# Layer 0 of a four-layer convolution network: x in pairs of patch rows, and one load for both the first block and the first image's statistics

## The chip, the cores and the metric

The kernel runs on one core of a Trainium2 chip. The metric is the device time of one execution in microseconds (us), as the median of several executions. All times before the change are of the same kernel file, and "the profile" is one execution of it that was recorded by the hardware profiler.

## The reference

Four residual layers follow each other on a tensor x of shape (4, 64, 256, 256), float32. Only layer 0 is touched:

```python
x = x + _L0_conv_ref(_gn(x), w_in, w_dw, fft_filter, w_out)   # layer 0
x = x + _L1_conv_ref(_gn(x), kernel)                          # layer 1
x = x + _L2_conv_ref(_gn(x), core, periphery, threshold, scale, 1, 1)
x = x + _L3_conv_ref(_gn(x), weights1, weights2)

def _L0_conv_ref(x, w_in, w_dw, fft_filter, w_out):           # p = 8
    x = jnp.einsum('bchw,oc->bohw', x, w_in)                  # 64 -> 384 channels
    xp = x.reshape(B, C, H // p, p, W // p, p).transpose(0, 1, 2, 4, 3, 5)
    xf = jnp.fft.rfft2(xp) * fft_filter                       # per 8x8 patch
    xp = jnp.fft.irfft2(xf, s=(p, p))
    x = xp.transpose(0, 1, 2, 4, 3, 5).reshape(B, C, H, W)
    x = lax.conv_general_dilated(x, w_dw, (1, 1), [(1, 1), (1, 1)], feature_group_count=C)
    x1, x2 = jnp.split(x, 2, axis=1)
    return jnp.einsum('bchw,oc->bohw', jax.nn.gelu(x1, approximate=False) * x2, w_out)
```

`_gn` subtracts the mean of a group of two channels over a whole image and divides by the root of its variance, so nothing of an image can be normalized before the whole image has been read once.

## The kernel before, in words

**Start.** The 256 image rows are 32 patch rows of 8 rows each. The statistics of image 0 are read in 32 parts of 512 KB (`first_stats`, L663). Tensor `flat` lays each part over all 128 partitions: partition 2c+s holds half s of channel c, 4096 bytes in a run, one DMA for a part. Seven buffers (`p_s`) rotate, so part k+7 is asked for when part k has been read. VectorE reads each part with two `bn_stats` (`input_stats`, L320). Between them stands, at k = 0, 10 and 20, the building of the depthwise-and-FFT weights: `tables` on VectorE (L339 to L352), copies into the tiles `T` on ScalarE and GpSimd (L391) and twelve writes of `T` to HBM from GpSimd's queue (L395). Then `group_norm` gives scale and shift; as `flat` mixes channels differently from the working layout it uses two averaging matrices (`c_avgp`, `c_avgx`). Tile `u` takes the memory of the weight tiles when these are done.

**Blocks.** An image is three blocks of 11 output patch rows; twelve blocks in all. A block needs patch rows i0 to i0+11, of which one is shared with the block before it. i0 is -1, 10 or 21, so the first block of an image has no row t = 0 and the last one has no row t = 11. `load_x` reads one patch row as two DMAs (L418): partitions 0 to 63 get the left half of the image's width, 64 to 127 the right half, in runs of 512 bytes. `normalize_x` scales it into a tile `xn` (L256 on ScalarE; in block 0 every other row on GpSimd, L425).

**The four passes of a block.** For each of four groups kb of 96 hidden channels the kernel first expands (`expand`) every patch row t into `u`, then runs the patch convolution on `u` (`own` L498, `beside` L514) for twelve pairs of channel groups g, with GELU on ScalarE (L521), the product on VectorE (L522) and the result to HBM (L525, tile `g`). An expand step has two forms: for t < 6 ("pairs") 16 matmuls of 128 weights columns (L446) and four copies on each of ScalarE and VectorE (L461); for t of 6 and more 32 matmuls of 64 columns (L452) and three copies on each (L463 to L465). The profile counts each matmul twice[...].

**Units.** While block p convolves, the projection of block p-1 is done in 16 units (`project`, L602, L609), four in each pass, at g = 0, 4, 6, 8 in the pass kb = 0 and g = 0, 2, 6, 8 in the others. A unit adds into a residual tile `r` (loaded by `load_r`, L570) and asks for the next row's `r` and `g` (`load_half`, L557, L561).

**Order.** TensorE, VectorE, ScalarE and SyncE run in the order in which the program is written (`manual_schedule`); GpSimd's order follows from it. All loads of layer 0 stand on SyncE's queue (SP), which waits in order for the buffers it loads into. `load_w` (L473, four buffers) waits for TensorE and so keeps SP in step with the convolution. The statistics of the next image (L638) and the x of the next block share the four buffers `p_x`; in passes kb 0 to 2 up to four statistics parts a pass are loaded, at the end of kb = 2 four rows of x (g = 8 and g = 10), and in pass kb = 3 the next block's rows are normalized, three ahead of g = 0 and two after each pair of groups.

Of the kernel before, what the change touches and what calls it, by code (L numbers as in the profile page):

```python
# [17 lines left out]
C = 64  # L18
# [3 lines left out]
GROUPS = 32  # L22
# [47 lines left out]
def _constants(H, W):  # L70
# [4 lines left out]
    grpp = np.arange(128) // 2 // (C // GROUPS)  # L75
    avgp = (grpp[:, None] == grpp[None, :]) / np.sum(grp == 0)
    avgx = (grpp[:, None] == grp[None, :]) / np.sum(grp == 0)
# [10 lines left out]
        "c_ident": np.eye(128), "c_avg32": avg32, "c_sel32": sel32, "c_kext": _patch_kernel(), "c_avg": avg, "c_avgp": avgp, "c_avgx": avgx,  # L88
# [33 lines left out]
class _Net:  # L122
# [152 lines left out]
    def _layer0(self, ctx, dst):  # L275
# [32 lines left out]
        p_xn, p_x = pool("l0xn", NR + 1), pool("l0x", 4)  # L308
# [20 lines left out]
        p_s = ctx_a.enter_context(tc.tile_pool(name="l0as", bufs=7))  # L329
# [46 lines left out]
        def weights(t, copies):  # L376
# [33 lines left out]
        rows_of = lambda p: [  # L410
            (blocks[p][0], blocks[p][1] + t) for t in range(NR + 1) if 0 <= blocks[p][1] + t < NP
        ]

        def load_x(row, p_x=p_x):
            b, i = row
            x0[row] = p_x.tile([128, P, HW2], F32, tag="x", name=f"x0_{b}_{i}")
            for s in range(2):
                nc.sync.dma_start(x0[row][halves[s]], a["x"][b, :, P * i : P * i + P, s * HW2 : (s + 1) * HW2])  # L418

        def normalize_x(row, pool=False):  # L420
            b, i = row
            xn = xns[row] = p_xn.tile([128, HW2 // P, P, P], F32, tag="xn", name=f"xn_{b}_{i}")
            to, x = xn.rearrange("p m r w -> p r m w"), x0.pop(row).rearrange("p r (m w) -> p r m w", w=P)
            if pool:
                nc.gpsimd.tensor_scalar(to, x, self.r[0][:, b : b + 1], self.nb[0][:, b : b + 1], ALU.mult, ALU.add)  # L425
            else:
                self.normalize(to, x, 0, b)
# [6 lines left out]
        def expand(p, kb, t):  # L434

            b, i0 = blocks[p]
            ps = [banks(f"psu_{p}_{kb}_{t}_{s}") for s in range(2)]
            xn = xns[b, i0 + t]
            lo, hi = halves
            pairs = t < (NR + 1) // 2  # L440
# [15 lines left out]
            at = lambda h, o: u[h, :, t * CW + o : t * CW + o + 8].rearrange("p c (s m) -> p c s m", s=2)  # L456
            for s, copy in enumerate((nc.scalar.copy, nc.vector.tensor_copy)):
                v = ps[s][:, :, 0 : 8 * PB].rearrange("p s (m c) -> p c s m", m=4)
                if pairs:
                    for h, o, k, c in ((lo, O1, lo, 0), (hi, O2, lo, PB), (lo, E1 + 1, hi, 0), (hi, E2 + 1, hi, PB)):  # L460
                        copy(at(h, 8 * s + o), v[k, c : c + PB])  # L461
                    continue
                copy(at(slice(0, 128), 8 * s + 1), v[:, 0:PB])  # L463
                copy(at(hi, 8 * s + E2 + 1), v[lo, PB:])
                copy(at(lo, 8 * s + O1), v[hi, PB:])  # L465
# [186 lines left out]
        with ordered:  # L652

            bst0 = new_bst0(0)
            flat = a["x"][0].rearrange("c (s h) w -> (c s) (h w)", s=2)
            avgs = [self.load(name, p_a) for name in ("c_avgp", "c_avgx")]
            parts = {}

            def first_stats(k):
                if k >= NJ:  # L660
                    return
                t = parts[k] = p_s.tile([128, 4, W], F32, tag="x", name=f"st_{k}")
                nc.sync.dma_start(t.rearrange("p r w -> p (r w)"), flat[:, 4 * W * k : 4 * W * (k + 1)])  # L663
# [5 lines left out]
            for k in range(7):  # L669
                first_stats(k)  # L670
            copies = [nc.scalar.copy, nc.gpsimd.tensor_copy, nc.scalar.copy]
            for k in range(NJ):
# [4 lines left out]
                first_stats(k + 7)  # L677
            rows = rows_of(0)
            for row in rows[:4]:
                load_x(row)  # L680
            for j in range(3):
                load_w(j)
            self.group_norm(0, 0, bst0, avgs)
            ctx_a.close()

            p_1, p_6 = (pool(n, 2, side="right") for n in ("l0g1", "l0g6"))
            p_r = pool("l0r", 2, side="right")
# [3 lines left out]
            sources = [[p_1, p_6, p_r]]  # L691
# [831 lines left out]
```

## Time and profile before

| what | value |
|---|---|
| median of three runs (lowest, highest) | 6424.22 us (6414.56, 6427.8) |
| the profiled execution: its own time / its span | 6435.86 us / 6434.0 us |
| TensorE matmul busy | 5962.3 us, 93% of the span |
| VectorE / ScalarE / GpSimd busy | 4271.5 / 3239.1 / 1058.2 us |
| moved by DMA | 1448.20 MB, mean 225 GB/s, 879566 packets |
| statistics of image 0 end on VectorE (start of L200) | 90.42 us |
| first normalized row starts on ScalarE (L256) | 99.54 us |
| first expand matmul of block 0 (L446) | 100.83 us |
| convolution of block 0 runs without gaps from (L498) | 149.72 us |

Times in the views are counted from the start of the span. A timeline line gives start, duration, engine, source line, operation, output and inputs, how many instructions were merged, and in brackets how long the engine had been idle before it and what ended that. In a table of stretches the columns are start:end, length, busy time of each engine with its instructions, the TensorE clock that was granted, the share of the 16 DMA engines' time that was busy, and GB/s. A line of waits gives the total in us, how often, and the longest. "issue" is a wait for nothing that the profile shows.

### The profile page before, as it was taken

The numbers are of one execution on the slowest core, as the hardware profiler recorded it, in microseconds if no ns is written. First come the engines' busy times: TensorE is split into PE (matmuls) and PEld (weight loads), VectorE is DVE, ScalarE is ACT, GpSimd is POOL, SyncE is SP. The second block draws the span as 40 slices with busy tenths as digits, with TensorE's granted clock in tenths as the row PEclk, the third lists the DMA queues.
The fourth block names the chain that finished last, engine by engine and source line by source line (L and its number), as shares of the span: only waits on it lengthen the run. The fifth ranks groups of instructions, "written<-read, shape, count | busy, mean of one in ns | idle before, by whom it ended". The sixth has DMA issues, their size and how long they took to land.

```text
span 6434.0 us, 238132 instructions
## 1 busy us (share of the span) xinstructions
PE 5962.3 (93%) x106712; PEld 3313.0 (51%) x106712; DVE 4271.5 (66%) x5924; ACT 3239.1 (50%) x4560; POOL 1058.2 (16%) x1651
## 2 busy tenths in 40 slices
PE   3999999999999999999999969999899999999997
PEld 2565555555555555555565533333344444443566
DVE  5566565565666565655565538999788988885264
ACT  3454444444344444343444406777777877773211
POOL 4111111111111111111111111111122222221011
PEclk9999999999999999999999979999999999999855
DMA  8587888888888878887877699999566666678899
GB/s 237 161 216 217 225 234 240 240 230 227 243 225 236 228 210 236 239 233 219 227 207 211 196 233 240 229 228 229 139 174 176 177 169 172 169 187 286 302 365 393
DMA packets 879566, 1448.20 MB, mean 225 GB/s; under 512 B 77284, under 2 KB 587508, under 8 KB 876500
## 3 DMA queue, kind: packets, MB, share of 16 engines
q1 hardware_dynamic: 726340, 923.62, 55.7%
q0 software_dynamic: 148672, 500.14, 23.0%
q8 instruction: 843, 13.81, 0.9%
q10 hardware_dynamic: 3536, 9.20, 0.6%
q14 instruction: 175, 1.43, 0.1%
HBM read 932.61 MB, written 500.04 MB: 223 GB/s over the span
## 4 chain that ended last, share of the span: by engine, by line
PE 76%; DMA 9%; DVE 8%; ACT 3%; issue 3%; SPq 0%; POOL 0%; DVEq 0%; ACTq 0%; POOLq 0%
PE pc L514 16%; PE pc L498 11%; PE m L906 10%; PE one L1147 9%; PE div L1106 7%; DVE u L461 5%; PE psu L446 5%; PE psu L452 5%; PE po L602 4%; DMA g<-g 2%; PE psz L1136 2%; DMA x<-in_x_dram 2%; PE po L609 2%; DMA x<-x 2%; PE psa L1334 2%
## 5 line engine op out<-in xcount | busy, mean ns | idle before, releaser
L522 DVE TENSOR_TENSOR h<-h,pc 128x374 f32<-128x374 f32 x1152 | 575.7, 541 | 1171.1 <-ACT h L521 1171.0
L521 ACT ACTIVATE h<-pc 128x374 f32<-128x374 f32 x1152 | 494.0, 480 | 1649.4 <-PE pc L514 1649.0
L514 PE MATMUL pc<-u,w 64*16 64x374 f32 (+2 forms) x27648 | 1179.3, 479 | 1.9 <-issue 1.9
L525 POOL DMA_DIRECT2D g<-h x576 | 418.4, 726 | 2874.5 <-DVE h L522 2784.7
L498 PE MATMUL pc<-u,w 64*64 64x374 f32 x9216 | 828.8, 483 | 14.0 <-DVE r L623 5.1
L514 PEld LDWEIGHTS pc<-u,w 64*16 64x16 f32 (+2 forms) x27648 | 466.8, 92 | 678.8 <-issue 638.0
L461 DVE COPY u<-psu 64x384 f32<-64x384 f32 x1088 | 605.0, 556 | 60.6 <-PE psu L446 42.5
L1092 DVE TENSOR_TENSOR q<-xn 128x2313 f32<-128x2313 f32 (+2 forms) x256 | 627.6, 2493 | 1.7 <-ACT xn L256 1.7
L446 PE MATMUL psu<-win,xn 64*128 64x96 f32 x8704 | 588.7, 279 | 42.0 <-ACT u L461 21.6
L461 ACT COPY u<-psu 64x384 f32<-64x384 f32 x1088 | 559.3, 514 | 115.5 <-PE psu L446 90.8
L1147 PE MATMUL one<-z,wp 32*32 32x512 f32 x16384 | 595.7, 597 | 21.7 <-issue 17.5
L452 PE MATMUL psu<-win,xn 64*64 64x96 f32 x17408 | 502.0, 256 | 118.2 <-issue 75.2
L446 PEld LDWEIGHTS psu<-win,xn 64*128 64x128 f32 x8704 | 553.7, 190 | 97.8 <-DVE h L522 30.7
L256 ACT ACTIVATE xn<-x,nb,r 128x1024 f32<-128x1024 f32 (+3 forms) x268 | 478.4, 1799 | 246.0 <-DMA x<-x 140.4
L498 PEld LDWEIGHTS pc<-u,w 64*64 64x64 f32 x9216 | 360.4, 132 | 389.0 <-issue 165.7
L1093 ACT ACTIVATE q<-q 128x2313 f32<-128x2313 f32 (+2 forms) x256 | 528.9, 2086 | 31.9 <-DVE q L1092 31.0
L452 PEld LDWEIGHTS psu<-win,xn 64*64 64x64 f32 x17408 | 438.6, 140 | 176.7 <-issue 101.3
L1147 PEld LDWEIGHTS one<-z,wp 32*32 32x32 f32 x16384 | 368.2, 103 | 229.9 <-issue 88.2
L1106 PE MATMUL div<-q,ones 64*32 64x512 f32 x8192 | 471.0, 601 | 10.1 <-ACT q L1093 9.3
L1180 POOL DMA_DIRECT2D x<-r x512 | 274.3, 544 | 980.0 <-DVE r L1177 946.8
L602 PE MATMUL po<-g,wo 128*64 128x176 f32 (+1 forms) x3072 | 320.1, 351 | 75.6 <-DMA g<-g 51.3
L906 PE MATMUL m<-t,wk 64*64 64x512 f32 x3072 | 341.2, 588 | 0.0
(163 smaller groups left out, 6703.2 us busy)
## 6 DMA issues: line engine op xcount, KB each, us to landing
g<-h POOLq DMA_DIRECT2D x576, 374.0 KB, 6.9
x<-x SPq DMA_DIRECT2D x240, 640.0 KB, 6.5
w<-wt SPq DMA_DIRECT2D x288, 448.0 KB, 6.7
x<-x SPq DMA_DIRECT2D x100, 1024.0 KB, 14.3
g<-g SPq DMA_DIRECT2D x414, 187.0 KB, 6.5
g<-g SPq DMA_DIRECT2D x736, 93.5 KB, 6.0
x<-in_x_dram SPq DMA_DIRECT2D x258, 256.0 KB, 8.6
x<-o POOLq DMA_DIRECT2D x128, 512.0 KB, 8.3
```

What stands on the lines that cost most here:

```text
L446: nc.tensor.matmul(ps[s][:, k, at], xn[halves[s], n : n + 2].rearrange("p n r w -> p (n r w)"), win[halves[s], kb, 0 : 2 * PB], start=True ...
L452: nc.tensor.matmul(ps[s][halves[1 - odd], k, at], xn[halves[s], n + odd].rearrange("p r w -> p (r w)"), win[halves[s], kb, PB * (1 - odd) ...
L461: copy(at(h, 8 * s + o), v[k, c : c + PB])
L498: nc.tensor.matmul(out(C * c, C, k, h), w[halves[h], k, 2 * (G % 2) + c, 0:C], cells(h, 4 * g + 2 * k + c, 0, 0), start=True, stop=False, ...
L514: nc.tensor.matmul(out(q, m, k, h), w[halves[h], k, 2 * (G % 2) + c, c0 : c0 + m], cells(h, 4 * g + 2 * k + c, down, right), start=False, ...
L522: nc.vector.tensor_mul(h[:, k], h[:, k], ps[k][:, 1, 0:L])
L602: nc.tensor.matmul(out(k, s, x), wo1, moving(g1[:, 2 * k], 2 * half + k, s, x), start=(x == 0), stop=False, skip_group_check=True,)
L906: nc.tensor.matmul(rows2(m)[halves[j], s], w[dx][halves[s]], ts[n][halves[s], i, 2 * j : 2 * j + 2, dx : dx + W], start=(dx == 0), stop=(d ...
L1092: nc.vector.tensor_sub(d, p0, p1)
L1093: nc.scalar.activation(d, d, AF.Square)
L1106: ins = nc.tensor.matmul(ps[quarters[j], h], ones[halves[h]], q[n, g, k][halves[h], r + 2 * j : r + 2 * j + 2, o : o + W], start=(m == 0), ...
L1147: ins = nc.tensor.matmul(rows2(ps[g])[quarters[j], k], w[quarters[i]], z[quarters[i], h, 2 * j + dy : 2 * j + dy + 2, dx : dx + W], tile_p ...
```

## The change

**Layout of x.** A part of x is now four image rows of two neighbouring patch rows: partitions 0 to 63 hold rows of patch row i, partitions 64 to 127 the same rows of patch row i+1, each over the whole width, 4096 bytes in a run. Two parts (k = 0, 1) make a pair of patch rows. The last patch row of a block (k = 2, the one shared with the next block) keeps the old layout, in a pool `p_x1` of its own. A part is 512 KB as before, in two DMAs of 64 partitions.

**Expand.** A step of a block is now the left or right half of a pair of patch rows, so a step fills half of two rows of `u` rather than one whole row. `pairs` goes by the number of the step in the block (under 6), not by t: a block with i0 = -1 now has six steps with pairs and five without, where it had five and six. The other two kinds of block keep their numbers (six and six, six and five).

**Start.** The first ten statistics parts of image 0 are the ten parts of block 0 (`kept`), and stay in SBUF (four in `p_x`, six in a temporary pool `p_f`) until they are normalized. The other 22 parts rotate in three buffers, not seven, and are laid out like the later images' statistics: two DMAs of 64 partitions a part. All 32 parts have the working layout, so `group_norm` uses one matrix. The reload of block 0's rows is gone, but for the shared row (k = 2). Two parts on ScalarE and two on GpSimd are normalized before the first step, and one more at each later step.

**Loads.** The first unit in pass kb = 0 moves from g = 0 to g = 4 (now g = 4, 6, 8, 10). The first two `load_half` move from t = 0 and t = 11 to t = 11 and g = 0, and the `load_r` of the first row from the end of the block before to step t = 0. Two of the four x loads at the end of pass kb = 2 move into pass kb = 3, behind its expand steps.

```diff
-        p_xn, p_x = pool("l0xn", NR + 1), pool("l0x", 4)
+        p_xn, p_x1, p_x = pool("l0xn", NR // 2), pool("l0x1", 2), pool("l0x", 4)
...
-        p_s = ctx_a.enter_context(tc.tile_pool(name="l0as", bufs=7))
+        p_s = ctx_a.enter_context(tc.tile_pool(name="l0as", bufs=3))
+        ctx_f = ExitStack()
+        p_f = ctx_f.enter_context(tc.tile_pool(name="l0f", bufs=6, side="right"))
...
+        def parts_of(p):
+            b, i0 = blocks[p]
+            out = [(b, i0 + 1 + 2 * m, k) for m in range(NR // 2) for k in range(2)]
+            return out + ([(b, i0 + NR, 2)] if i0 + NR < NP else [])
+        def load_x(part, p_x=p_x):
+            b, i, k = part
+            x0[part] = t = p_x.tile([128, 4, W], F32, tag="x", name=f"x0_{b}_{i}_{k}")
             for s in range(2):
-                nc.sync.dma_start(x0[row][halves[s]], a["x"][b, :, P * i : P * i + P, s * HW2 : (s + 1) * HW2])
+                if k < 2:
+                    nc.sync.dma_start(t[halves[s]], a["x"][b, :, P * (i + s) + 4 * k : P * (i + s) + 4 * k + 4, :])
...
+        def steps_of(p):
+            b, i0 = blocks[p]
+            one = lambda t: [(b, i0 + t, 0, [(t, 0), (t, 1)])] if 0 <= i0 + t < NP else []
+            out = one(0)
+            for t in range(1, NR, 2):
+                out += [(b, i0 + t, q, [(t, q), (t + 1, q)]) for q in range(2)]
+            return out + one(NR)
-        def expand(p, kb, t):
-            pairs = t < (NR + 1) // 2
+        def expand(p, kb, step, pairs):
+            b, i, q, to = step
+            xn = xns[b, i][:, 16 * q : 16 * q + 16]
...
             for s, copy in enumerate((nc.scalar.copy, nc.vector.tensor_copy)):
+                o0 = to[s][0] * CW + 8 * to[s][1]
...
-            flat = a["x"][0].rearrange("c (s h) w -> (c s) (h w)", s=2)
-            avgs = [self.load(name, p_a) for name in ("c_avgp", "c_avgx")]
+            first_parts = parts_of(0)
+            kept, parts = first_parts[: 2 * (NR // 2)], {}
             def first_stats(k):
+                if k < len(kept):
+                    load_x(kept[k], p_x if k < 4 else p_f)
+                    parts[k] = x0[kept[k]]
+                    return
                 t = parts[k] = p_s.tile([128, 4, W], F32, tag="x", name=f"st_{k}")
-                nc.sync.dma_start(t.rearrange("p r w -> p (r w)"), flat[:, 4 * W * k : 4 * W * (k + 1)])
+                for s in range(2):
+                    nc.sync.dma_start(t[halves[s]], src_t[0, :, k, s])
...
-            for k in range(7):
+            for k in range(len(kept) + 3):
                 first_stats(k)
...
-                first_stats(k + 7)
-            rows = rows_of(0)
-            for row in rows[:4]:
-                load_x(row)
+                if k >= len(kept):
+                    first_stats(k + 3)
...
-            self.group_norm(0, 0, bst0, avgs)
+            self.group_norm(0, 0, bst0)
...
                 def load_next(kb):
-                    if kb < 3 and nk:
+                    if kb == 3:
+                        load_rows(2)
+                    elif nk:
...
                     for t in range(NR + 1):
+                        if p == 0 and kb == 0:
+                            if t == 1:
+                                for part in first_parts[len(kept) :]:
+                                    load_x(part)
+                            for n in range(4) if t == 0 else range(t + 3, t + 4):
+                                if n < len(first_parts):
+                                    normalize_x(first_parts[n], pool=n % 2 == 1)
+                        if t < len(steps):
+                            expand(p, kb, steps[t], t < (NR + 1) // 2)
+                        if t == 0 and kb == 0 and 0 < p:
+                            load_r(p - 1, 0)
-                        if t in (0, NR) and first:
-                            load_half(*first.pop(0))
                         if t == NR:
+                            if first:
+                                load_half(*first.pop(0))
                             load_w(p * (HID // 8) + NG * kb // 2 + 3)
                             load_next(kb)
...
-                        if g in (0, 2 if kb else 4, 6, 8):
+                        if g in ((0, 2, 6, 8) if kb else (4, 6, 8, 10)):
                             unit()
-                        if g < 6:
+                        if g == 0 and first:
+                            load_half(*first.pop(0))
+                        if g < 6 and kb < 3:
                             load_next(kb)
...
-                            if g == NG - 2 and p < NB - 1:
-                                load_r(p, 0)
...
-                        if kb == 2 and g >= NG - 4:
+                        if kb == 2 and g == NG - 2:
                             load_rows(2)
```

## The prediction

> **What bounds the kernel now.** I read the page first, then the timeline of the first 155 us, then TensorE's waits and its timeline inside layer 0, then tables of short stretches for the DMA rates.
>
> ```profile
> PE 5962.3 (93%) x106712; PEld 3313.0 (51%) x106712; DVE 4271.5 (66%) x5924; ACT 3239.1 (50%) x4560; POOL 1058.2 (16%) x1651
> ...
> PE 76%; DMA 9%; DVE 8%; ACT 3%; issue 3%; SPq 0%; POOL 0%; DVEq 0%; ACTq 0%; POOLq 0%
> ```
>
> TensorE is the bound nearly everywhere. So a change of loads can gain only where TensorE stands still: at the start, and in short gaps inside the blocks.
>
> ```profile
> 6.47 64.82 SPq L663 DMA_DIRECT2D st<-in_x_dram  x32
> ...
> 47.94 1.29 DVE L320 BATCH_NORM_STATS2 bst<-st 128x6 f32<-128x512 f32 x2 [3.54 <-DMA st<-in_x_dram]
> ...
> 71.35 29.18 SPq L418 DMA_DIRECT2D x<-in_x_dram  x8
> ...
> 90.42 1.89 DVE L200 BATCH_NORM_AGGREGATE mv<-bst 128x2 f32<-128x384 f32 x1
> ...
> 99.54 1.24 ACT L256 ACTIVATE xn<-x,nb,r 128x1024 f32<-128x1024 f32 x1 [19.29 <-DMA x<-in_x_dram]
> ...
> 149.72 2.81 PE L498 MATMUL pc<-u,w 64*64 64x374 f32 x28 [1.22 <-DVE u L465]
> ```
>
> The statistics wait for their DMAs and end at 90.4 us; ScalarE then waits for x that is read a second time, and block 0's first expand pass (100.83 to 149.72, 49 us) goes row by row with these loads. The same pass in kb = 1 takes 25 us.
>
> ```profile
> PE psu L452 <- issue: 66.3, 49, 5.7
> ```
>
> ```profile
> 722.75 2.95 PE L452 MATMUL psu<-win,xn 64*64 64x96 f32 x64 [4.93 <-issue]
> ```
>
> ```profile
> q1 hardware_dynamic: 2162, 2.32, 87.4%
> q8 instruction: 3, 0.05, 1.7%
> ```
>
> Inside the blocks the largest gap of TensorE is no data wait: 66.3 us of "issue" in the expand steps with 64-column matmuls. The last two lines are the DMA view of 711 to 724 us, around the gap that the timeline line shows: loads fill the engines while instruction packets of 16 KB come on queue 8. I read it as late instructions; it is an inference. From the timeline, gaps over 0.9 us add up to 3.9 us a block in pass kb = 0, 1.9 in kb = 3, and almost nothing in the two others.
>
> [...]in 110 to 120 us the granted clock is 0.66 and 64 matmuls take 6.73 us, against 3.81 later.
>
> ```profile
> 9.00:20.00 11.00, 0.00 (x0) 0.00 (x0) 11.00 (x19) 5.42 (x27) 7.75 (x20) 1.00 1.00 390
> 121.00:129.00 8.00, 6.42 (x96) 6.06 (x96) 3.55 (x7) 3.50 (x8) 1.20 (x1) 0.61 0.88 180
> 131.00:138.00 7.00, 4.31 (x123) 4.12 (x119) 3.34 (x6) 4.19 (x7) 0.00 (x0) 0.74 0.61 152
> ```
>
> The last two columns are the busy share of the DMA engines and GB/s. Statistics parts over 128 partitions: 390 GB/s with all engines busy. Rows of x in two halves, 512-byte runs: 180 / 0.88 = 205. Statistics parts of image 1 in two halves, 4096-byte runs: 152 / 0.61 = 249. So the longer run is worth a fifth, and the half-wide tile costs a third or more. The new layout is the third row, and it also replaces the first.
>
> **The change part by part.**
>
> *Statistics stage, slower.* A part took 0.524 MB / 390 = 1.34 us alone and, from the stats starting at 47.94, 50.63 and 53.19, 2.6 us beside the writes of T. In halves it takes 0.524 / 249 = 2.1 us alone. Beside the writes it lies between 2.6 (the writes are the limit) and 2.6 x 390 / 249 = 4.1 (all of it is the halves); I take 3.0. Parts 0 to 5 land by 20 us, part 9 at 20 + 4.5 x 3.0 = 33.5, so the second `tables` (9.7 us long, from 26.34 before) runs 34.7 to 44.4. With three buffers only parts 10 to 12 are loaded meanwhile. Part 13 is asked for when part 10 is read (45.6), lands 3.5 + 1 us later (3.47 is the shortest landing of a half), then one per 3.0 us: part 19 is read at 69.7, `tables` ends at 79.4, part 23 lands at 85, part 31 at 109. Statistics end at 110 instead of 90.4. With 2.6 us a part the same walk gives 102, with 3.6 it gives 121; above that the writes run out and the reads speed up.
>
> *Start of block 0, faster.* From the end of the statistics to scale and shift took 5.3 us (90.4 to 95.7); two matmuls and a copy less, 5.0. GpSimd's queue then holds the memset of u (1.47) ahead of its first normalization (1.20), and the first step needs both parts: TensorE starts 7.7 us after the statistics. The pass has six steps with pairs and five without: ScalarE does 6 x 2.13 + 5 x 1.54 of copies and four normalizations of 1.24 between them, 25.4 us, after a cold first step of 3.3: 29 us, where x loads made it 49. The convolution starts at 110 + 7.7 + 29 = 146.7, 3.0 us earlier than 149.72 (bounds: 11 earlier, 8 later). The reload of 5.2 MB that is saved pays for the slower reads and little more.
>
> *Expand form, slower.* In four blocks one step of eleven changes from three copies and 64-column matmuls to four copies and 128-column ones. The timeline prices them:
>
> ```profile
> 1160.47 6.81 PE L446 MATMUL psu<-win,xn 64*128 64x96 f32 x96 [0.48 <-ACT u L461]
> ...
> 1171.61 6.73 PE L452 MATMUL psu<-win,xn 64*64 64x96 f32 x252 [0.17 <-DVE u L465]
> ```
>
> Three pair steps take 6.81 + 0.08 of overlap, 2.28 a step (VectorE's four copies of 0.556 are 2.22); four of the other kind take 6.73, 1.7 to 1.85 with their waits. So 0.45 us x 15 passes (block 0's first is in the sum above) = 7 us more; from 4 to 13, since whole passes with six pairs end 23.2 to 23.4 us after their start and those with five 22.1 to 22.7.
>
> *Unit moved from g = 0 to g = 4, faster.* Gaps of the convolution in pass kb = 0 of blocks 1 to 10 add up to 6.7 us; with g loaded half a pass earlier most of them go: 4 us less (0 to 6). VectorE's adds (1.46 + 0.80 + 0.80) move beside matmuls either way.
>
> *Loads inside blocks.* 110 of the 117 later rows of x change from 512 to 4096 bytes, about a fifth less engine time on 58 MB of the 668 MB that the DMA view counts from 100 to 3100 us. SP issues as many DMAs. Moved on SP: `load_r` of the first row passes only g loads that wait for the block's last `g` write, so it starts when it did; the `r` of the second row leaves the crowded expand of kb = 0, while a statistics part enters it; two x parts in kb = 3 now stand behind a `load_w` that waits for TensorE to end the pass before, so they land within the expand rather than ahead of it. Who waits behind them: the normalization at g = 0, some 20 us later, which a landing of 8 to 13 us leaves room for. For the late instructions I take 5 us less, between 33 less (half of 66) and 22 more (kb = 3 gets gaps like kb = 0's, 2.0 more in 11 blocks).
>
> *Costed at nothing:* the normalization's new write order (runs of 8 floats as before, 1.24 us); `p_f` and the later pools over it (first used in block 1). Layers 1 to 3 only start earlier or later.
>
> **Sum.** -3 + 7 - 4 - 5 = -5 us on the profiled 6435.86 us (span 6434.0). That execution lies 11.6 us above the median of the runs; I carry the difference to the median: 6424.2 - 5 = 6419 us. About 0.2% (13 us) is what a measurement here can tell from no change.
>
> **Rivals.**
> - *Instruction gaps shrink by half* (faster): x in 4096-byte runs and the second `r` out of the way. -3 + 7 - 4 - 33 = -33: 6391 us. For it: nearly every long gap of kb = 0 follows `r` and statistics loads. Against: as many bytes are moved in the same passes.
> - *The x parts moved into kb = 3 collide with its 64-column steps* (slower). Place: the second half of that expand, where instructions are used up fastest. Price: 2.0 us x 11 = 22, without the 5 saved: -3 + 7 - 4 + 22 = +22, 6446 us. It decides from (13 + 0) / 11 = 1.2 us a block on. For it: the gaps of kb = 3 already follow x loads. Against: half of these loads stood close by before.
> - *The halves cost little at the start or a lot:* at 3.6 us a part, 121 instead of 110: +11 on the sum, 6430 us. This is also the case in which the change does not do what it says, since the longer runs then buy nothing.
>
> **Chances.** Likeliest case 0.45 (own range 6404 to 6434), gaps halve 0.25, collision 0.20, slow statistics 0.10. Faster: 0.25 and an eighth of the likeliest case, 0.30. Slower: 0.20 and some of the two middle cases, 0.26. Range 6386 to 6448, which leaves out the far ends of both outer rivals.
>
> **What would show it.** Right: L200 starts near 110 us (102 to 121), `st` and first x DMAs at about 250 GB/s when alone, the first pass of block 0 some 29 us long without x waits on ScalarE, its convolution at about 147; L446 rises from 8704 to 9216 matmuls; "issue" at the 64-column line near 60 us. Wrong: L200 before 98[...], or "issue" under 35 or over 80.

## The result and the profile after

The kernel after takes 6440.15 us (median of 20 runs, 6424.17 to 6447.08), the kernel before on the same chip 6421.69 us (20 runs, 6407.66 to 6440.3). The ratio is 1.0026, 95% interval 1.0019 to 1.0034: slower by 0.26%, some 17 us. The profiled execution has a span of 6445.2 us against 6434.0.

The page of after, engines and chain:

```profile
PE 5961.0 (92%) x106198; PEld 3303.0 (51%) x106198; DVE 4282.4 (66%) x5939; ACT 3245.7 (50%) x4575; POOL 1059.0 (16%) x1651
...
PE 76%; issue 7%; DVE 7%; DMA 6%; ACT 3%; POOL 1%; SPq 0%; POOLq 0%; DVEq 0%; ACTq 0%
```

TensorE does the same work in the same busy time. So the loss is again in its waits, and in the chain the share of DMA has even fallen (9% to 6%) while that of issue rose (3% to 7%).

The timeline of the start of after (L317 reads the parts, L692 loads the 22 that are not kept, L197 ends the statistics):

```profile
5.54 15.85 SPq L422 DMA_DIRECT2D x<-in_x_dram  x20
22.02 90.15 SPq L692 DMA_DIRECT2D st<-in_x_dram  x44
...
41.20 3.65 DVE L317 BATCH_NORM_STATS2 bst<-st 128x6 f32<-128x512 f32 x6
49.68 1.29 DVE L317 BATCH_NORM_STATS2 bst<-st 128x6 f32<-128x512 f32 x2 [4.82 <-DMA st<-in_x_dram]
...
62.02 1.29 DVE L317 BATCH_NORM_STATS2 bst<-st 128x6 f32<-128x512 f32 x2 [5.64 <-DMA st<-in_x_dram]
...
73.34 1.29 DVE L317 BATCH_NORM_STATS2 bst<-st 128x6 f32<-128x512 f32 x2 [3.42 <-DMA st<-in_x_dram]
...
90.02 1.28 DVE L317 BATCH_NORM_STATS2 bst<-st 128x6 f32<-128x512 f32 x2 [2.15 <-DMA st<-in_x_dram]
...
118.68 1.29 DVE L317 BATCH_NORM_STATS2 bst<-st 128x6 f32<-128x512 f32 x2 [1.27 <-DMA st<-in_x_dram]
120.00 1.89 DVE L197 BATCH_NORM_AGGREGATE mv<-bst 128x2 f32<-128x384 f32 x1
...
157.65 2.81 PE L523 MATMUL pc<-u,w 64*64 64x374 f32 x28 [0.81 <-DVE u L490]
```

The statistics end at 120.0 us (before 90.4). Block 0's first expand pass then takes 30 us where it took 49, and its convolution runs without gaps from 157.65, 7.9 us later than before. Alone, the parts in two halves came about as fast as forecast, 241 GB/s against 249 (last two columns: busy share of the DMA engines, GB/s):

```profile
9.00:20.00 11.00, 0.00 (x0) 0.00 (x0) 11.00 (x18) 5.21 (x27) 7.66 (x20) 1.00 1.03 241
```

For the blocks I took from TensorE's timeline, for each pass, the time from its first expand matmul to its first convolution or projection matmul, and from there to the next pass. The table has the means of blocks 1 to 9 in us:

| kernel | kb = 0 | kb = 1 | kb = 2 | kb = 3 | block |
|---|---|---|---|---|---|
| before | 28.3 + 51.0 | 24.0 + 50.4 | 23.8 + 50.5 | 26.8 + 50.9 | 305.7 |
| after | 28.4 + 54.3 | 25.4 + 50.3 | 23.8 + 50.3 | 24.4 + 49.4 | 306.1 |

So two things of about equal size cancel in each block: kb = 0 and 1 lose 4.7 us, kb = 3 gains 4.0. TensorE's waits between 100 and 3100 us in after name the loss (in the columns: total, times, longest):

```profile
PE psu L476 <- issue: 47.4, 45, 3.1
PE psu L470 <- ACT u L486: 21.0, 42, 1.3
PE pc L523 <- DVE u L490: 18.1, 18, 2.0
PE pc L539 <- issue: 11.1, 9, 2.2
```

"Issue" at the 64-column matmuls fell from 66.3 to 47.4. The third line is new in this size (3.9 before): the convolution's first matmuls wait for VectorE's last copy into `u`. So is the fourth (1.9 before), a wait inside the convolution for nothing that the profile shows.

### The profile page after: what moved, and what is told of

Same layout as the page of the kernel before. It is cut to its first block, busy times and chain, and to the rows that moved or that the text cites. A ratio compares the mean times of both kernels' runs of the same rounds, so it can differ in the third digit from the quotient of the medians.

```text
span 6445.2 us, 237146 instructions
## 1 busy us (share of the span) xinstructions
PE 5961.0 (92%) x106198; PEld 3303.0 (51%) x106198; DVE 4282.4 (66%) x5939; ACT 3245.7 (50%) x4575; POOL 1059.0 (16%) x1651
## 4 chain that ended last, share of the span: by engine, by line
PE 76%; issue 7%; DVE 7%; DMA 6%; ACT 3%; POOL 1%; SPq 0%; POOLq 0%; DVEq 0%; ACTq 0%
PE pc L539 17%; PE pc L523 11%; PE m L940 10%; PE one L1181 9%; PE div L1140 7%; PE psu L470 4%; DVE u L486 4%; PE psu L476 4%; PE po L627 4%; PE psz L1170 2%; PE po L634 2%; DMA x<-x 2%; PE psa L1368 2%; ACT u L486 1%; DMA g<-g 1%
## 5 line engine op out<-in xcount | busy, mean ns | idle before, releaser
L539 PE MATMUL pc<-u,w 64*16 64x374 f32 (+2 forms) x27648 | 1186.2, 479 | 12.5 <-issue 12.5
L523 PE MATMUL pc<-u,w 64*64 64x374 f32 x9216 | 835.8, 485 | 28.3 <-DVE u L490 21.1
L539 PEld LDWEIGHTS pc<-u,w 64*16 64x16 f32 (+2 forms) x27648 | 465.7, 92 | 698.5 <-issue 664.1
L486 DVE COPY u<-psu 64x384 f32<-64x384 f32 x1152 | 640.1, 556 | 50.6 <-PE psu L470 31.3
L470 PE MATMUL psu<-win,xn 64*128 64x96 f32 x9216 | 618.3, 277 | 36.1 <-ACT u L486 24.9
L486 ACT COPY u<-psu 64x384 f32<-64x384 f32 x1152 | 592.3, 514 | 109.8 <-PE psu L470 78.7
L470 PEld LDWEIGHTS psu<-win,xn 64*128 64x128 f32 x9216 | 582.0, 188 | 93.3 <-ACT u L486 33.6
L476 PE MATMUL psu<-win,xn 64*64 64x96 f32 x16384 | 468.5, 253 | 89.0 <-issue 55.3
L476 PEld LDWEIGHTS psu<-win,xn 64*64 64x64 f32 x16384 | 407.3, 138 | 145.7 <-issue 83.2
L627 PE MATMUL po<-g,wo 128*64 128x176 f32 (+1 forms) x3072 | 316.3, 348 | 64.8 <-DMA g<-g 37.9
```

Of the source, the lines that this page charges most:

```text
L470: nc.tensor.matmul(ps[s][:, k, at], xn[halves[s], n : n + 2].rearrange("p n r w -> p (n r w)"), win[halves[s], kb, 0 : 2 * PB], start=True ...
L476: nc.tensor.matmul(ps[s][halves[1 - odd], k, at], xn[halves[s], n + odd].rearrange("p r w -> p (r w)"), win[halves[s], kb, PB * (1 - odd) ...
L486: copy(at(h, o0 + o), v[k, c : c + PB])
L523: nc.tensor.matmul(out(C * c, C, k, h), w[halves[h], k, 2 * (G % 2) + c, 0:C], cells(h, 4 * g + 2 * k + c, 0, 0), start=True, stop=False, ...
L539: nc.tensor.matmul(out(q, m, k, h), w[halves[h], k, 2 * (G % 2) + c, c0 : c0 + m], cells(h, 4 * g + 2 * k + c, down, right), start=False, ...
L627: nc.tensor.matmul(out(k, s, x), wo1, moving(g1[:, 2 * k], 2 * half + k, s, x), start=(x == 0), stop=False, skip_group_check=True,)
```

## The experiments

Each kernel was timed beside the kernel before on its own chip, in five rounds. The chips differ by 0.4% (before took 6421 to 6445 us), so kernels are compared with after by the quotient of their ratios; its uncertainty is some 0.15%, or 10 us. My theory: the start is slower because the half-wide loads are slow, and moving the unit uncovers the copies into `u`. Rivals: the loss is in the blocks alone (pairs form, instruction gaps); only the number of buffers counts at the start.

| kernel | ratio to before (95%) | against after, us |
|---|---|---|
| one DMA a part (`e_one_start`) | 1.0388 (1.037 to 1.0407) | +232 |
| eight parts ahead (`e_deep`) | 0.9986 (0.9976 to 0.9996) | -26 |
| unit back at g = 0 (`e_unit0`) | 0.9959 (0.9946 to 0.9973) | -43 |
| five pairs where it had five (`e_pairs`) | 1.0027 (1.0015 to 1.0039) | +1 |
| before, unit moved (`b_unit_only`) | 1.0069 (1.0054 to 1.0084) | |
| before, halves (`b_halves`) | 1.0026 (1.0014 to 1.0037) | |
| both repairs (`e_best`) | 0.9921 (0.9907 to 0.9936) | -67 |
| fill in one quarter (`e_fill`) | 1.0074 (1.006 to 1.0088) | +31 |
| fill in four quarters (`e_fill2`) | 1.0005 (0.9995 to 1.0014) | -13 |
| x loads early (`e_xearly`) | 1.0031 (1.0021 to 1.004) | +3 |
| three pairs (`e_pairs3`) | 1.0074 (1.006 to 1.0087) | +31 |
| all pairs (`e_allpairs`) | 1.0094 (1.0081 to 1.0108) | +44 |
| after, short runs (`e_short`) | 1.0059 (1.0046 to 1.0072) | +21 |
| before, long runs (`b_long`) | 0.9956 (0.9942 to 0.9969) | |

### The start: halves or buffers

`e_one_start`:

```diff
+        def load_both(t, b, row, apart):
+            v = a["x"][b, :, row : row + 4, :]
+            src = bass.AP(tensor=v.tensor, offset=v.offset, ap=[[apart * W, 2], [H * W, C], [1, 4 * W]])
+            nc.sync.dma_start(t.rearrange("p r w -> p (r w)"), src)
...
-                for s in range(2):
-                    nc.sync.dma_start(t[halves[s]], src_t[0, :, k, s])
+                load_both(t, 0, 8 * k, 4)
```

> The kernel after, with one edit: each of the 32 statistics parts of image 0, the ten kept ones included, is read by one DMA over all 128 partitions and not by two of 64; places, buffers (three) and everything else stay. My theory (halves are what makes the statistics stage slow): the statistics end at 94 to 100 us, not at 120.0, block 0's convolution runs from about 135, not 157.65, and the time falls by about 20 us (15 to 25) below the kernel after, to about its 6420. Rival (only the small number of buffers holds the stage up, halves cost nothing): the statistics still end after 112 us and the time falls by at most 6 us. Rival (the loss lies in the blocks alone): the stage may get shorter, the time stays within 5 us of the kernel after.

All three expectations failed. The timeline and a table of two stretches of this kernel:

```profile
97.39 237.85 SPq L420 DMA_DIRECT2D st<-in_x_dram  x22
```

```profile
60.00:90.00 30.00, 0.00 (x0) 0.00 (x0) 3.86 (x6) 0.00 (x0) 0.00 (x0) 1.00 0.13 52
100.00:130.00 30.00, 0.00 (x0) 0.00 (x0) 11.44 (x24) 0.00 (x0) 0.00 (x0) 1.00 0.13 52
```

A part now takes some 10 us: 52 GB/s, with 0.13 of the 16 engines' time busy, as much as two engines have. The kernel before reads a part by one DMA too, and did so at 390 GB/s with a share of 1.00. Its source begins with a dimension of 128 and the one here with a dimension of 2; that this makes the difference was not shown. Since whole parts were that slow here, this run tells nothing about halves; the next two do.

`e_deep` keeps the halves and, in place of `p_s`, lends them five tiles of `p_xn`, which are idle at that time:

```diff
-                t = parts[k] = p_s.tile([128, 4, W], F32, tag="x", name=f"st_{k}")
+                if k % 2 == 0:
+                    parts["two"] = p_xn.tile([128, 2, 4, W], F32, tag="xn", name=f"st_{k}")
+                t = parts[k] = parts["two"][:, k % 2]
...
-                    first_stats(k + 3)
+                    first_stats(k + 8)
```

> The kernel after, with one edit: the 22 statistics parts that are not kept rotate in five tiles of two parts each (eight parts asked for ahead) and not in three single buffers; the two half-wide DMAs a part stay. My theory (halves cost most of it, few buffers a part): the statistics end at 104 to 110 us, not at 120.0, and the time falls by about 13 us (8 to 16). Rival (only the buffers): they end at 90 to 96 us and the time falls by 25 us or more. Rival (blocks alone): the time stays within 5 us.

`b_halves` gives the kernel before, with its seven buffers, the half-wide parts:

```diff
-                nc.sync.dma_start(t.rearrange("p r w -> p (r w)"), flat[:, 4 * W * k : 4 * W * (k + 1)])
+                for s in range(2):
+                    nc.sync.dma_start(t[halves[s]], src_t[0, :, k, s])
...
-            self.group_norm(0, 0, bst0, avgs)
+            self.group_norm(0, 0, bst0)
```

> The kernel before, with one part of the change alone: the 32 statistics parts of image 0 are read in two DMAs of 64 partitions each; seven buffers, the reload of x and all else stay. My theory as it stands after the run with eight parts ahead (that one ended its statistics at 95.5 us with the same halves): the halves alone cost little, the statistics end at 93 to 99 us (before: 90.4) and the time grows by 2 to 8 us. Rival (what I predicted blind, a part in 3.0 us beside the writes whatever the buffers): they end after 105 us and the time grows by 15 us or more.

The end of the statistics in `e_deep`, then in `b_halves`, with parts of the latter beside the writes of T:

```profile
95.48 1.89 DVE L197 BATCH_NORM_AGGREGATE mv<-bst 128x2 f32<-128x384 f32 x1
```

```profile
50.92 1.29 DVE L320 BATCH_NORM_STATS2 bst<-st 128x6 f32<-128x512 f32 x2 [2.90 <-DMA st<-in_x_dram]
52.92 1.29 DVE L320 BATCH_NORM_STATS2 bst<-st 128x6 f32<-128x512 f32 x2 [0.71 <-DMA st<-in_x_dram]
54.87 1.29 DVE L320 BATCH_NORM_STATS2 bst<-st 128x6 f32<-128x512 f32 x2 [0.66 <-DMA st<-in_x_dram]
57.67 1.29 DVE L320 BATCH_NORM_STATS2 bst<-st 128x6 f32<-128x512 f32 x2 [1.51 <-DMA st<-in_x_dram]
60.73 1.29 DVE L320 BATCH_NORM_STATS2 bst<-st 128x6 f32<-128x512 f32 x2 [1.78 <-DMA st<-in_x_dram]
...
95.41 1.89 DVE L200 BATCH_NORM_AGGREGATE mv<-bst 128x2 f32<-128x384 f32 x1
```

With seven buffers the halves cost 5.0 us of the 29.6 (95.4 against 90.4), and a part comes every 2.45 us beside the writes (60.73 - 50.92 over four). With three buffers it came every 3.6 to 3.9 us (49.68 to 73.34 in six steps, 90.02 to 118.68 in eight), though the halves are the same. The number in flight sets that: in after a part lands 7.9 us after its issue (median), its read takes 1.3, the issue of its two DMAs 1.2, so by my estimate three buffers give one part in 10.4 / 3 = 3.5 us. And while `tables` holds VectorE for 9.7 us, only three parts come, twice (the line at 41.20 reads them, two `bn_stats` a part). In the kernel before it was seven and then five, as its timeline has it:

```profile
36.01 8.40 DVE L320 BATCH_NORM_STATS2 bst<-st 128x6 f32<-128x512 f32 x14
...
64.08 6.26 DVE L320 BATCH_NORM_STATS2 bst<-st 128x6 f32<-128x512 f32 x10
```

So the rival on the buffers had it (an end between 90 and 96 us, 25 us or more saved), but for those 5.0 us; my theory on the halves failed.

The time of `b_halves` grew by 17 us, of which the start explains 5.5 (block 0 begins at 106.32, not at 100.83). The rest lies in blocks that the edit doesn't touch, and stays open; its runs scatter from 6446 to 6484 us.

### The unit

`e_unit0`:

```diff
-                        if g in ((0, 2, 6, 8) if kb else (4, 6, 8, 10)):
+                        if g in (0, 2 if kb else 4, 6, 8):
```

with `load_half` and `load_r` back where they stood.

> The kernel after, with one edit: the first projection unit of pass kb = 0 is back at g = 0 (now 0, 4, 6, 8 as before the change), with the places of the first load_half and of load_r that went with it. My theory (without the unit TensorE waits at the start of each kb = 0 convolution for the last copies of u): the convolution of pass kb = 0 falls from 54.3 to about 51 us a block, the expand pass of kb = 1 by about 1 us, and the time by 25 to 45 us. Rival (the loss in the blocks is the pair form and instruction gaps that go elsewhere): the wait at the first convolution matmuls shrinks, but kb = 3 or kb = 0's expand grow by as much; the time stays within 8 us. What I predicted blind for the move was a gain of 4 us, so undoing it would cost 4.

`b_unit_only` makes the opposite edit in the kernel before and moves no load.

> The kernel before, with one part of the change alone: the first unit of pass kb = 0 moves from g = 0 to g = 4 (4, 6, 8, 10); the loads stay where they stood. My theory (undoing it in the kernel after gave the first 32 matmuls of the convolution 2.8 us in place of 2.0 of waiting and 4.5): the convolution of kb = 0 grows from 51.0 to about 54.4 us a block, the time by 35 to 42 us over the kernel before (ratio about 1.006). Rival (the loads that were moved with it did it): the convolution of kb = 0 stays within 1 us of 51.0 and the time within 8 us. What I predicted blind: a gain of 4 us.

Means of a block as in the table above:

| kernel | kb = 0 | kb = 1 | kb = 2 | kb = 3 | block |
|---|---|---|---|---|---|
| `e_unit0` | 29.1 + 50.9 | 23.6 + 50.5 | 23.8 + 50.1 | 25.2 + 49.5 | 302.6 |
| `b_unit_only` | 29.4 + 54.5 | 24.9 + 50.6 | 23.7 + 50.3 | 26.7 + 51.2 | 311.1 |

`b_unit_only` took 44 us more than before. Both kernels agree with my theory: the convolution of kb = 0 is about 3.5 us longer without a unit at g = 0, whichever kernel it is, and the pass kb = 1 is 1 to 2 us longer. The loads that moved with the unit are not the cause. TensorE at the border in block 2, first in after, then in `e_unit0` (L627 and L634 are the unit):

```profile
732.79 1.43 PE L476 MATMUL psu<-win,xn 64*64 64x96 f32 x56
736.22 4.46 PE L523 MATMUL pc<-u,w 64*64 64x374 f32 x32 [1.99 <-DVE u L490]
740.61 4.07 PE L539 MATMUL pc<-u,w 64*16 64x374 f32 x96
744.61 2.82 PE L523 MATMUL pc<-u,w 64*64 64x374 f32 x32
```

```profile
732.65 1.24 PE L476 MATMUL psu<-win,xn 64*64 64x96 f32 x20
733.82 2.05 PE L627 MATMUL po<-g,wo 128*64 128x176 f32 x16
735.80 0.93 PE L634 MATMUL po<-g,wo 64*64 64x176 f32 x16
736.55 2.77 PE L523 MATMUL pc<-u,w 64*64 64x374 f32 x32
```

The unit needs `g`, not `u`. So TensorE had 2.5 to 3 us of work in the time in which ScalarE and VectorE empty the last expand step into `u`. Without it there is a gap of 2 us. To see what that is worth, I split the pass kb = 0 behind the first 32 matmuls of its convolution (means of blocks 1 to 9 in us; the first column starts where the last expand matmul ends):

| kernel | up to the 32nd matmul | rest of the pass |
|---|---|---|
| before, unit inside | 5.6 | 45.3 |
| `e_unit0`, unit inside | 5.5 | 45.4 |
| after | 5.4 | 49.5 |
| `b_unit_only` | 5.4 | 49.7 |

In the wait the unit cost nothing that this table shows. In its new place the rest of the pass is over 4 us longer: 2.3 to 2.5 us are the unit itself, 1.1 are further gaps of TensorE (0.7 us a block in `e_unit0`, 1.8 in after; the waits for issue at L539 are 1.4 us in `e_unit0` and 11.1 in after), and the remainder is not placed.

In block 2 the 32 matmuls behind the gap also take 4.46 us instead of 2.8. The stretches of after show the granted clock there (third column from the right):

```profile
736.00:738.00 2.00, 1.78 (x16) 1.13 (x20) 0.00 (x0) 0.00 (x0) 0.00 (x0) 0.67 0.00 0
738.00:740.00 2.00, 2.00 (x16) 1.03 (x12) 0.00 (x0) 0.00 (x0) 0.00 (x0) 0.50 0.00 0
740.00:742.00 2.00, 2.00 (x48) 0.68 (x48) 0.00 (x0) 0.00 (x0) 0.00 (x0) 0.97 0.04 8
```

The longest gap in the 13 us before was 2.3 us, the one right ahead of these matmuls 2.0. But the half clock came right behind such a gap at only three of the eleven borders. By the clock in the trace of after, only in blocks 2, 5 and 8 did the first 32 matmuls run at half clock (0.50) for a part or the whole of their time, and in block 11 the same gap is followed by full speed:

```profile
3478.75 2.82 PE L523 MATMUL pc<-u,w 64*64 64x374 f32 x32 [2.00 <-DVE u L490]
```

From 395 to 3150 us the half clock was granted for 54.6 us in after and for 59.9 us in `e_unit0`. So the slow clock is not what makes the moved unit dear.

Two kernels were built on the belief that the slow clock is nearly half of the loss. They fill the gap with matmuls that nobody uses.

`e_fill`:

```diff
+                        if g == 0 and kb == 0 and p > 0:
+                            ps, xn = banks(f"fill_{p}"), xns[steps[-1][:2]]
+                            for n in range(32):
+                                nc.tensor.matmul(ps[halves[0], 0, 0 : 2 * PB],
+                                    xn[halves[0], n % 16].rearrange("p r w -> p (r w)"),
+                                    win[halves[0], kb, 0 : 2 * PB], start=True, stop=True)
```

> The kernel after, with work added: ahead of the first convolution matmul of kb = 0 in blocks 1 to 11 TensorE does 32 more matmuls of the 64-column kind into a bank that nobody reads (1.66 us of work, which computes nothing that is used). My theory (the unit at g = 0 filled a wait of 2.0 us for the last copies of u, and without it TensorE also runs the next matmuls at half clock): the convolution starts when it did, but its first 32 matmuls take about 2.8 us and not 4.46, so that 11 x 1.6 = 18 us are gained in spite of the added work (10 to 20). Rival (only the wait counts, the slow matmuls have another cause): no gain, within 4 us of the kernel after, or up to 5 slower.

`e_fill2` has the same 32 matmuls with `ps[halves[n % 2], s, ...]`, `xn[halves[s], n]` and `win[halves[s], ...]`.

> As the last kernel but with the 32 added matmuls spread over the four quarters of the array as an expand step does it, so that they take 1.66 us and not the 4.4 us that they took with all in one quarter (they compute nothing that is used). My theory: they end before the last copy of u, the convolution starts when it did in the kernel after, its first 32 matmuls take 2.8 us and not 4.46, and the time falls by 11 x 1.6 = 18 us (10 to 20) below the kernel after: ratio to before about 0.9998. Rival (the matmuls are slow for another reason, or the wait grows): within 4 us of the kernel after (1.0026) or slower.

Border of block 2, `e_fill` and then `e_fill2`:

```profile
735.80 4.37 PE L817 MATMUL fill<-win,xn 64*64 64x96 f32 x51
...
740.09 2.67 PE L523 MATMUL pc<-u,w 64*64 64x374 f32 x29
```

```profile
730.61 1.47 PE L818 MATMUL fill<-win,xn 64*64 64x96 f32 x60 [0.52 <-issue]
...
731.98 2.76 PE L523 MATMUL pc<-u,w 64*64 64x374 f32 x31
734.68 4.07 PE L539 MATMUL pc<-u,w 64*16 64x374 f32 x96
```

In `e_fill` I had priced the filling wrongly: all in one quarter of the array the matmuls take more than 4 us, so the convolution starts too late, and the kernel loses 31 us, though the convolution's first matmuls are fast (2.67 us). The 32 matmuls took 4.4 us in one 64 x 64 quarter and 1.5 to 1.7 us over four; since `e_fill2` also spreads its results over two banks, it was not shown which of the two made the difference.

In `e_fill2` useless work made the kernel 13 us faster (10 to 20 expected, but with an uncertainty of some 10). The stretch up to the 32nd matmul falls from 5.4 to 5.0 us, most of it in the three slow blocks (6.5, 6.5 and 7.3 us in after; 5.2, 5.6 and 5.4 here). That is some 4 us in eleven blocks, and I take it as the slow clock's part. Where the rest of the 13 us lies is not shown.

### The form of the expand steps

`e_pairs`, `e_pairs3` and `e_allpairs` change one number, the step up to which the pairs form goes:

```diff
-                            expand(p, kb, steps[t], t < (NR + 1) // 2)
+                            expand(p, kb, steps[t], t < (NR + 1) // 2 - (i0 < 0))   # or t < 3, or True
```

> The kernel after, with one edit: blocks with i0 = -1 have five steps in the pairs form and six in the other, as before the change, and not six and five. My theory and the prediction's term: 15 passes get 0.45 us shorter each, 7 us in all (4 to 13), with L470's matmuls back at 8704. Rival (a pair step costs what the other one costs, since late instructions take the difference): within 3 us of the kernel after.

> The kernel after, with one size changed: the pairs form for the first three steps of every pass and not for six. The prediction's price of a pair step (0.45 us more than the other form): 3 steps x 44 passes x 0.45 = 59 us less. Rival (the other form has twice the matmuls and so more late instructions, as the run with five pairs hints, which gained nothing): between 10 us less and slower.

> The kernel after, with one size changed: all steps of a pass in the pairs form. The prediction's price: 5.3 steps x 44 passes x 0.45 = 105 us more. Rival (the issue gaps of the other form, some 55 us, go with it): 50 us more, and the waits for issue in the expand lines fall below 20 us.

TensorE's waits for issue at expand lines, 100 to 3100 us, in `e_pairs3` (L476: 64 columns) and in `e_allpairs` (L470: pairs):

```profile
PE psu L476 <- issue: 114.7, 77, 4.4
```

```profile
PE psu L470 <- issue: 2.2, 6, 0.8
```

One step more or less in four blocks can't be measured (1 us, with an uncertainty of 10). Fewer pairs cost 31 us and more pairs 44 us: of the numbers tried, six is the best or as good. A step without pairs saves copies but has twice the matmuls, and its issue gaps grow from 47.4 to 114.7 us with three steps more a pass. With pairs alone these gaps are gone, but each step has four copies instead of three on both engines, and the rival's 50 us more was nearer than the 105 of my price, which saw only the copies.

### What pass kb = 3 gained

`e_xearly` loads the two x parts at the end of kb = 2 again:

```diff
-                    if kb == 3:
-                        load_rows(2)
-                    elif nk:
+                    if kb < 3 and nk:
...
-                        if kb == 2 and g == NG - 2:
+                        if kb == 2 and g >= NG - 4:
```

> The kernel after, with one edit: the two x parts that moved into pass kb = 3 are loaded at the end of kb = 2 again (four at g = 8 and 10). The pass kb = 3 took 77.7 us a block before and 73.7 after. Theory A (the new place of these loads brought that gain, the opposite of my rival): kb = 3 grows by 2 us or more a block, the time by 20 us or more. Theory B (the runs of 4096 bytes and the moved unit loads brought it): kb = 3 within 1 us, the time within 8 us. My rival of the prediction (they collide): the time falls by 10 us or more.

It took 24.9 + 49.3 us in kb = 3 (after: 24.4 + 49.4), and 3 us more in all: the place of these loads has no effect that can be measured. With place and form tried, the length of the runs was left. `e_short`:

```diff
-                if k < 2:
+                if k < 2 and (b, i, k) in first_parts:
```

so that all other parts take the branch with 512-byte runs. And `b_long`, in the kernel before, reads x in runs of 4096 bytes:

```diff
-                nc.sync.dma_start(x0[row][halves[s]], a["x"][b, :, P * i : P * i + P, s * HW2 : (s + 1) * HW2])
+                nc.sync.dma_start(x0[row][halves[s]].rearrange("p r w -> p (r w)"),
+                    a["x"][b, :, P * i + 4 * s : P * i + 4 * s + 4, :].rearrange("c r w -> c (r w)"))
```

In both, as many bytes and DMAs go into the same tiles, but the tiles hold other pixels than the layer needs.

> The kernel after, with one edit: the x parts of all blocks but the first are read in runs of 512 bytes, as the rows of the kernel before were (a patch row's two halves, as many bytes and DMAs into the same tiles); they hold other pixels, so layer 0 works on changed values. Theory A (the longer runs gave the 3 us a block that pass kb = 3 is shorter than before once the unit is back): kb = 3 grows from 73.7 to about 76.7 us a block and the time by 33 us (20 to 40) over the kernel after. Theory B (the runs don't matter; the other moves did it): kb = 3 within 1 us, the time within 8 us of the kernel after (1.0026).

> The kernel before, with one edit: x is read in runs of 4096 bytes (four image rows over the whole width for each half of a tile, as many bytes and DMAs into the same tiles); the tiles hold other pixels, so layer 0 works on changed values. Theory A: kb = 3 falls from 77.7 to about 74.7 us a block, the first pass of block 0 by a few us, and the time by 33 us (20 to 45) below the kernel before. Theory B: kb = 3 within 1 us, the time within 8 us of the kernel before.

| kernel | kb = 0 | kb = 1 | kb = 2 | kb = 3 | block |
|---|---|---|---|---|---|
| `e_short` | 27.8 + 54.3 | 25.0 + 50.6 | 23.9 + 50.4 | 26.6 + 51.0 | 309.5 |
| `b_long` | 29.0 + 50.9 | 24.0 + 50.1 | 23.8 + 50.3 | 25.6 + 49.4 | 303.0 |

The runs did it: taken away, kb = 3 is as long as before (77.6) and the kernel loses 21 us; given to the kernel before, kb = 3 falls to 75.0 and the kernel gains 28 us. ScalarE's waits for x from 395 to 3150 us go with them, in before, after, `e_short` and `b_long`:

```profile
ACT xn L256 <- DMA x<-in_x_dram: 72.6, 38, 4.7
```

```profile
ACT xn L253 <- DMA x<-in_x_dram: 23.5, 18, 1.9
```

```profile
ACT xn L253 <- DMA x<-in_x_dram: 62.1, 32, 4.1
```

```profile
ACT xn L256 <- DMA x<-in_x_dram: 20.8, 19, 1.9
```

In kb = 3 these normalizations stand ahead of the GELU on ScalarE, and between before and after TensorE's gaps in that convolution fall from 1.1 us a block to 0.1. In the expand pass they fall from 3.5 to 1.8 us (gaps over 0.1 us), and the time at half clock there from 3.0 us a block to none, which by my estimate is worth at most half of that (at half clock 32 matmuls took 4.46 us, not 2.8). Together this is about the gain of 4.0. That ScalarE's wait or the rows of x in the DMA engines cause the gaps of the expand pass is likely, but was not shown.

### Both repairs together

`e_best` has the edits of `e_deep` and `e_unit0`.

> The kernel after, with two edits that were each run alone: eight statistics parts ahead in two-part tiles, and the first unit of kb = 0 back at g = 0 with its loads. If the two losses are independent: ratio to the kernel before about 0.9986 x 0.9959 / 1.0026 = 0.992, some 52 us faster than before and 68 faster than after. Rival (the earlier start is eaten by something later in the blocks): above 0.996.

It takes 6394.08 us where before took 6444.89: 0.8% faster than before and 1.0% faster than after, and the two repairs add up as expected. Its start has a new limit:

```profile
92.33 1.89 DVE L197 BATCH_NORM_AGGREGATE mv<-bst 128x2 f32<-128x384 f32 x1
97.23 2.37 ACT L253 ACTIVATE xn<-x,nb,r 128x1024 f32<-128x1024 f32 x2 [16.62 <-DVE nb L218]
103.44 1.47 POOL L760 MEMSET u<- 128x1632 f32 x1 [6.44 <-DMA wt<-T]
...
106.14 8.27 PE L469 MATMUL psu<-win,xn 64*128 64x96 f32 x96 [9.99 <-POOL xn L440]
```

The memset of `u`, whose memory T still holds until its writes are done, now stands ahead of GpSimd's normalization, and TensorE starts 13.8 us after the statistics instead of 7.5.

## Why the prediction was wrong

I forecast -5 us, and the ratio says +17. The step that failed most is the moved unit, which I gave as a gain of 4 us and which costs some 38 to 43. By the steps:

- **Statistics stage, slower: the size failed.** "Beside the writes ... I take 3.0" became 3.6 to 3.9 us, and the end 120.0 instead of 110. I scaled the bandwidth of the half-wide tile and used the three buffers only for what is loaded during `tables`. But with three buffers a part's own latency sets its rate; the same halves come every 2.45 us with seven. My rival of slow statistics had 121 us, but that number came from another cause: it blamed the halves, which cost 5.0 of the 29.6 us. What followed was right: 7.5 us to the first matmul (7.7 forecast) and a first pass of 30 us (29). So the convolution of block 0 came 7.9 us later, not 3.0 earlier, inside the bound of 8.
- **Half-wide transfers: the reading failed.** From my third row (249 GB/s against 390) I took that the half-wide tile costs a third or more, and carried a part of that cost over to the time beside the writes of T. Alone it holds, since after shows 241. But beside the writes a part in halves came as often (2.45 us in `b_halves`) as a whole one (2.6 us in before), so there the price was an estimate that failed.
- **Unit moved from g = 0 to g = 4, faster: the sign failed.** I counted 4 us of gain in the unit's waits for `g`. I did not ask what the unit covers: it was TensorE's only work that does not need the last copies of `u`. Undoing the move gains 43 us; from the blocks, 3.5 us x 11 = 38.
- **Expand form, slower: the size failed.** +7 forecast, 0 measured within 10: the price came from stretches without issue gaps, and those go the other way.
- **Loads inside blocks: the sign was right, the size was not.** I took 5 us of the 33 that I gave as the end of the range; the longer runs are worth 21 to 28 us by the times. From the blocks, all that differs between before and `e_unit0` is worth (305.7 - 302.6) x 11 = 34. The rival with -33 had the size, without having the place or the mechanism: nearly all of it is in kb = 3, where x is normalized, and "issue" at the 64-column line fell by 19 us, not by half.
- **The collision of the x parts in kb = 3 did not come**: 3 us, no effect that can be measured.

Block 1 starts 7 us later than before. With the terms from the blocks the sum is 7 (start) + 38 (unit) - 34 (runs and the rest) = +11, the difference of the two spans (6445.2 - 6434.0). This is bookkeeping more than proof, since the last two terms are parts of one measured difference of blocks. That the total came within 22 us of the forecast is luck: two terms of over 30 us, of which I saw neither in its size, nearly cancel.

Several of the signs that I had named for being right came true: 120.0 lies within 102 to 121, 241 GB/s near 250, 30 us near 29, and the pairs form has 9216 matmuls. None of them looked at the moved unit.

## What to carry to other kernels

Before an independent piece of work is moved, ask which wait it fills: in the wait for `u` the unit was as good as free (5.5 to 5.6 us up to the 32nd matmul with it, 5.4 without), elsewhere it cost its own 2.3 to 2.5 us and the gaps that came with it. Where buffers are cut to make room, work out the rate as buffers over the time from issue to release too, and not from bandwidth alone. And price a change of form with the gaps that its instruction count brings (here 47.4 us of them became 114.7), not from busy stretches alone.

## What the hardware showed unexpectedly

A gap of 2.0 us on TensorE was followed in block 2 by a granted clock of 0.67 and 0.50 in two stretches of 2 us, and in block 11 by full speed. One DMA over all 128 partitions whose source begins with a dimension of 2 moved 52 GB/s, a fifth of the 241 that half-wide DMAs, two for each part, reached. Useless matmuls in the gap made the kernel 13 us faster, of which the slow clock explains some 4 by my estimate.
